# VectorE writes the inverse of the softmax totals itself, over all columns that carry it

## The chip, the cores and the metric

The kernel runs on one core of a Trainium2 chip. The metric is the device time of one execution in microseconds (us). Several executions are timed, and the median is given. One further execution is recorded by the profiler; all durations in this text come from that one.

## What is computed

The input x has 4 batches of 1024 positions with 256 values each, in fp32. Four blocks follow one another, each with a layer norm before it and a residual sum behind it: attention, a feed-forward network, a second attention, and the same feed-forward network again.

```python
x = x + _L0_attn_a_ref(_layernorm(x), kernel, WO)
x = x + _L0_ffn_ref(_layernorm(x), w1, b1, w2, b2)
x = x + _L0_attn_b_ref(_layernorm(x), w_down_q, w_down_kv, w_up_q, w_up_k, w_up_v, w_out, ln_scale, ln_bias)
x = x + _L0_ffn_ref(_layernorm(x), w1, b1, w2, b2)
```

Both attentions have 16 heads of 64 values and full rows of 1024 scores:

```python
scores = jnp.einsum('bhsd,bhtd->bhst', q, k) * scale
attn = jax.nn.softmax(scores, axis=-1)
out = jnp.einsum('bhst,bhtd->bhsd', attn, v)
```

The first makes q, k and v straight from the normed x. The second goes through two projections to 128 values, rotates q and k, and has a second norm. The softmax is what the change touches: each row of exponentials has to be divided by its total.

## The kernel before, in words

**Tiles.** Heads are worked on in pairs, and a pair of one batch takes 8 steps (`NT`), each of 128 positions as queries. With 4 batches and 8 pairs that is 256 steps for each attention layer, 512 in all. In one step there are two score tiles of 128 x 1024 (j = 0 and 1), in PSUM; the pool `ps_sc` has three such tiles. Score tile j holds the 128 queries of the pair's head j, one to a partition.

**One step, by engine.** TensorE makes the scores (`scores`, L247). VectorE takes each row's maximum, negated (`exponentials`, L258, two instructions a step). ScalarE makes the exponentials into the tile p and adds up each row's total into `total`, a tile of 128 x 2 (L260). The tile p has 17 groups (`NK`) of 128 columns: 16 carry exponentials, and the last one, p[:, NK2], carries the inverse of the totals, 64 columns for each of the two score tiles. `invert` fills that group: VectorE inverts the two totals in place (L268), and ScalarE copies each of them over its 64 columns (L269, read with a repeated element). Then VectorE transposes all 2176 columns of p in blocks of 32 x 32 into the tile T (`turn`, L280). Because the inverses are columns of p, they are transposed and moved together with the exponentials, and arrive lying along the axis along which they have to multiply.

**After the step.** Two steps (`HB`) share one T, called h. Its 16 blocks of 32 partitions are sent to their places in the tile pT by DMAs (`send`, L304): five are issued by GpSimd, the others by SyncE; SyncE has eleven per h in the first layer and ten in the second, where one block that need not change its partitions is copied by ScalarE instead (`keep`, L296). Five steps (`LAG`) later `weigh` (L313) multiplies pT by v on TensorE, `take` copies the sums to oT (ScalarE, L323) and multiplies them by the inverses that came along in pT (GpSimd, L325), and `project` (L176, L335, L337) applies the output weights and adds the result to x.

**Order.** The order on every engine is written out by hand in `steps_with`. In step s the program issues: `invert(s)`, `scores(s + 1)`, GpSimd's sends or `project` of an earlier h, the first maximum and exponentials of s + 1, other pieces of work that have a due step (projections of the next heads, norms), `weigh`, the second maximum and exponentials of s + 1, `take`, `turn(s)`, SyncE's sends. So VectorE's queue reads, step after step: inverse of s, two maxima of s + 1, transposition of s. Each engine works through its own queue in that order and waits at an instruction until what it needs is there. p, T and pT have two buffers each.

Between the two attention layers and at the end lie the feed-forward networks, which do not use `invert`.

The lines that the text names: L140 and L145 invert the spread of the norms (reciprocals of 128 x 4 to 128 x 24), L147 multiplies tiles of the same sizes by -1, L247 scores, L258 maxima, L260 exponentials, L268 and L269 the inversion, L280 the transposition, L304 the sends, L313 the weighing.

Of the kernel before, what the change touches and what calls it, by code (L numbers as in the profile page):

```python
# [48 lines left out]
def hybrid_block_kernel(  # L49
# [5 lines left out]
    nc = tc.nc  # L55
# [134 lines left out]
    def attention(prep_batch, prep_pair, wo, loader, lead, kept):  # L190
# [74 lines left out]

        def invert(s):
            t = total.pop(s)
            nc.vector.reciprocal(t, t)  # L268
            nc.scalar.copy(  # L269
                probs[s][:, NK2].rearrange("p (j c) i -> p j (c i)", j=2),  # L270
                t.unsqueeze(2).to_broadcast([P, 2, DH]),
            )
# [66 lines left out]
        def steps_with(others):  # L339
            for k, f in others:  # L340
                pieces.setdefault(k, []).append(f)
            for s in range(-1, n + LAG + 1):
                h, part = divmod(s - LAG, HB)
                ahead = 0 <= s + 1 < n
                if 0 <= s < n:
                    invert(s)
                if ahead:
                    scores(s + 1)
                if part == 1 and 0 <= s // HB - 1 < n // HB:
                    send(s // HB - 1, nc.gpsimd, sent[len(sent) - POOL_DMA :])  # L350
                if part == 1 and 0 <= h < n // HB:
                    project(h)
                if ahead:
                    exponentials(s + 1, 0)
                for f in pieces.get(s - EARLY, ()):
                    f()
                if part == 0 and 0 <= h < n // HB:
                    weigh(h)
                if ahead:
                    exponentials(s + 1, 1)  # L360
                if part == 0 and 0 <= h < n // HB:
                    take(h)
                if 0 <= s < n:
                    turn(s)
                if part == 0 and 0 <= s // HB - 1 < n // HB:
                    keep(s // HB - 1)
                    T.pop(s // HB - 1)
                if part == 0 and 0 <= s < n:
                    send(s // HB, nc.sync, sent[: len(sent) - POOL_DMA])
                for f in pieces.get(s, ()):  # L370
                    f()
# [597 lines left out]
```

## Time and profile before

| | |
|---|---|
| median of 3 runs | 3253.63 us (3250.37 to 3256.33) |
| the profiled execution | 3250.15 us, of which the span from first to last instruction is 3248.4 |
| granted TensorE clock | 0.996 of full speed |
| VectorE | 2723.5 us busy (84%), 2686 instructions |
| ScalarE | 2137.9 us busy (66%), 4400 instructions |
| TensorE | 3164.4 us busy (97%) |
| the inversion on VectorE (L268) | 512 x 130 ns = 66.7 us |
| the copy on ScalarE (L269) | 512 x 297 ns = 151.9 us |

PE is TensorE's matmul, PEld its loading of weights, DVE is VectorE, ACT ScalarE, POOL GpSimd, SP SyncE (its queue, SPq, issues DMAs). A group's row names the line, the engine, the operation, output<-inputs with shapes, and how often it occurs; then the busy time in us and the mean of one in ns; then how long the engine idled just before these instructions and what ended most of that idle time. Matmul times are modelled, so a busy TensorE is not necessarily one at its peak.

### The profile page before, as it was taken

To read this page: it belongs to the slowest core of one execution; us is meant where nothing else is said; L and a number is where in the kernel's file an instruction comes from. 1 tells how busy PE (TensorE), PEld (TensorE's weight loads), DVE (VectorE), ACT (ScalarE), POOL (GpSimd) and SP (SyncE) were. 2 spreads that over 40 slices of the span, in tenths; PEclk is the share of its full clock that TensorE was granted. 3 is DMA by queue.
4 is the path that set the end of the run, shared out by engine and by line. 5 is a ranking of instruction groups with operands and counts; after the bars stand their busy time and mean duration, and the time that the engine had idled before them with its cause. 6 is when DMAs were issued, how large, how long until landed. Compare 5 with 4: busy or idle time off the path is not lost.

```text
span 3248.4 us, 128967 instructions
## 1 busy us (share of the span) xinstructions
PE 3164.4 (97%) x53648; PEld 2092.2 (64%) x53648; DVE 2723.5 (84%) x2686; ACT 2137.9 (66%) x4400; POOL 2002.1 (62%) x2782
## 2 busy tenths in 40 slices
PE   8999999999999999999999999999999999999999
PEld 4666666666666666668866566666666666655688
DVE  7988888888888888966569989998999999999554
ACT  5666666666666666655447777777778777777542
POOL 4544545455444545442249889899899889886311
PEclk9999999999999999999999999999999999999999
DMA  8888888888888888850029889988989899988200
GB/s 228 217 224 215 224 224 228 217 219 222 221 217 225 219 231 223 221 150 1 4 74 244 225 228 243 242 237 236 246 243 243 234 240 246 238 235 221 57 20 27
DMA packets 244709, 642.29 MB, mean 198 GB/s; under 512 B 74304, under 2 KB 102976, under 8 KB 244128
## 3 DMA queue, kind: packets, MB, share of 16 engines
q1 hardware_dynamic: 161104, 397.60, 48.0%
q0 software_dynamic: 83024, 236.44, 26.0%
q8 instruction: 426, 6.98, 1.0%
q14 instruction: 155, 1.27, 0.1%
HBM read 43.39 MB, written 4.19 MB: 15 GB/s over the span
## 4 chain that ended last, share of the span: by engine, by line
PE 69%; SPq 12%; DMA 6%; DVE 5%; ACT 4%; issue 3%; POOL 1%; DVEq 0%; ACTq 0%; POOLq 0%
PE sc L247 20%; PE mm L313 19%; PE mm L176 15%; SPq L304 11%; DMA pT<-T 5%; PE pw L495 4%; PE mm L185 4%; PE mm L495 3%; PE mm L615 2%; DVE T L280 2%; DVE nmax L258 1%; ACT p L260 1%; PE ph L604 1%; ACT gT L529 1%; PE mm L162 1%
## 5 line engine op out<-in xcount | busy, mean ns | idle before, releaser
L258 DVE TENSOR_REDUCE nmax<-sc 128x1 f32<-128x1024 f32 x1024 | 1204.5, 1218 | 214.3 <-PE sc L247 211.3
L260 ACT ACTIVATE p<-sc,nmax 128x1024 f32<-128x1024 f32 x1024 | 1145.3, 1119 | 322.3 <-DVE nmax L258 322.2
L280 DVE STREAM_TRANSPOSE T<-p 128x2176 f32<-128x2176 f32 x512 | 1247.3, 2436 | 48.4 <-DMA pT<-T 18.4
L247 PE MATMUL sc<-kT,qT 64*64 64x512 f32 x8192 | 1082.5, 598 | 11.9 <-ACT p L260 10.3
L313 PEld LDWEIGHTS mm<-pT,v 64*64 64x64 f32 x32768 | 949.5, 133 | 140.7 <-issue 98.5
L313 PE MATMUL mm<-pT,v 64*64 64x128 f32 x32768 | 983.0, 269 | 9.6 <-issue 8.5
L304 POOL DMA_DIRECT2D pT<-T x1280 | 629.6, 499 | 125.5 <-PE sc L247 57.7
L325 POOL TENSOR_TENSOR oT<-oT,pT 128x256 f32<-128x256 f32 x256 | 187.0, 730 | 696.3 <-ACT oT L323 623.0
L247 PEld LDWEIGHTS sc<-kT,qT 64*64 64x64 f32 x8192 | 332.8, 133 | 401.6 <-issue 274.5
L337 POOL TENSOR_TENSOR x<-x,got 128x512 f32<-128x512 f32 x256 | 331.0, 1293 | 25.8 <-ACT got L335 22.0
L335 ACT COPY got<-mm 128x512 f32<-128x512 f32 x256 | 150.0, 586 | 281.8 <-PE mm L176 281.8
L176 PE MATMUL mm<-wo,oT 128*64 128x256 f32 x2048 | 279.9, 394 | 24.1 <-POOL oT L325 22.8
L176 PEld LDWEIGHTS mm<-wo,oT 128*64 128x64 f32 x2048 | 124.9, 136 | 273.2 <-POOL oT L325 226.5
L269 ACT COPY p<-total 128x128 f32<-128x128 f32 x512 | 151.9, 297 | 198.6 <-DVE total L268 192.4
L176 PE MATMUL mm<-hT,w 128*64 128x512 f32 x1024 | 243.4, 597 | 0.9 <-ACT hT L165 0.9
L260 ACT ACTIVATION_READ_ACCUMULATOR p<-sc,nmax 128x1 f32 x1024 | 205.2, 200 | 0.0
L185 PEld LDWEIGHTS mm<-w,hT 128*64 128x64 f32 x4096 | 140.9, 138 | 71.3 <-issue 69.4
L871 POOL TENSOR_TENSOR turned<-turned,sin_sb 128x512 f32<-128x512 f32 x128 | 163.8, 1279 | 0.0
L409 POOL TENSOR_TENSOR x<-x,b_sb 128x256 f32<-128x256 f32 x64 | 48.8, 777 | 170.6 <-ACT xn L156 170.6
L296 ACT COPY pT<-T 32x1088 f32<-32x1088 f32 x128 | 140.3, 1096 | 4.9 <-DMA pT<-T 1.1
L185 PE MATMUL mm<-w,hT 128*64 128x64 f32 x4096 | 140.9, 222 | 0.2 <-ACT kT L758 0.2
L176 PEld LDWEIGHTS mm<-hT,w 128*64 128x64 f32 x1024 | 73.3, 138 | 96.8 <-issue 75.0
(145 smaller groups left out, 2928.5 us busy)
## 6 DMA issues: line engine op xcount, KB each, us to landing
pT<-T SPq DMA_DIRECT2D x2688, 136.0 KB, 4.7
pT<-T POOLq DMA_DIRECT2D x1280, 136.0 KB, 4.7
turned<-kT POOLq DMA_DIRECT2D x128, 128.0 KB, 3.4
turned<-qT POOLq DMA_DIRECT2D x128, 128.0 KB, 3.5
w<-in_wqkv_a POOLq DMA_DIRECT2D x96, 128.0 KB, 6.0
wo<-in_wo_a POOLq DMA_DIRECT2D x32, 128.0 KB, 5.4
wo<-in_wo_a POOLq DMA_DIRECT2D x64, 64.0 KB, 5.5
wo<-in_wo_b SPq DMA_DIRECT2D x32, 128.0 KB, 4.0
```

The source lines that it names most:

```text
L176: nc.tensor.matmul(out[ts(j, DH)], lhsT[:, ts(j, DH)], rhs[j], start=(first and i == 0), stop=(last and i == len(parts) - 1),)
L185: nc.tensor.matmul(out[ts(j, DH)], lhsT, rhs[:, ts(j, DH)], start=(i == 0), stop=(i == len(parts) - 1),)
L247: nc.tensor.matmul(sc[s, j][ts(half, DH), ts(m, 512)], qT()[rows, ts(2 * qs + half, DH)], kT()[rows, ts(m, 512)], start=True, stop=True,)
L258: nc.vector.tensor_reduce(nmax, sc[s, j], AX.X, ALU.max, negate=True)
L260: nc.scalar.activation(probs[s][:, :NK2, ts(j, 2), :], sc.pop((s, j)).rearrange("p (k c i) -> p k c i", c=2, i=SQ), AF.Exp, bias=nmax, acc ...
L280: nc.vector.transpose(T[h][:, :, q, :, :].rearrange("p c k i -> p k c i"), probs.pop(s))
L304: engine.dma_start(pT[h][ts(c, SQ), a], T[h][ts(a, SQ), c])
L313: nc.tensor.matmul(av[h][q][ts(j ^ q, DH)], v[ts(j, DH), k, :], pT[h][ts(j, DH), :, q, k, :], start=(k == 0), stop=(k == NK2 - 1),)
L325: nc.gpsimd.tensor_mul(parts, parts, pT.pop(h)[:, :, :, NK2, :])
L337: nc.gpsimd.tensor_add(xd, xd, got)
L495: nc.tensor.matmul(bank[:, t, : right(k).shape[-1]], left(t, k), right(k), start=(first and t == 0 and k == 0), stop=(k == n_k - 1), skip_ ...
L871: nc.gpsimd.tensor_mul(other, other, sin_sb[:, ts(qb, QB)])
```

## The change

The reciprocal no longer overwrites the 128 x 2 tile of totals. It reads that tile with each element repeated 64 times and writes its results straight into the 128 columns of p. ScalarE's copy is gone.

```diff
         def invert(s):
             t = total.pop(s)
-            nc.vector.reciprocal(t, t)
-            nc.scalar.copy(
+            nc.vector.reciprocal(
                 probs[s][:, NK2].rearrange("p (j c) i -> p j (c i)", j=2),
                 t.unsqueeze(2).to_broadcast([P, 2, DH]),
             )
```

The place of the reciprocal in VectorE's queue is the same. Lines behind the change have numbers that are smaller by one.

## The prediction

> **What bounds the kernel now.** I read the page's busy table and chain first, then VectorE's groups by shape, then the two attention stages cut out as windows, and last VectorE's order of time inside them.
>
> ```profile
> span 3248.4 us, 128967 instructions
> PE 3164.4 (97%) x53648; PEld 2092.2 (64%) x53648; DVE 2723.5 (84%) x2686; ACT 2137.9 (66%) x4400; POOL 2002.1 (62%) x2782
> PE 69%; SPq 12%; DMA 6%; DVE 5%; ACT 4%; issue 3%; POOL 1%; DVEq 0%; ACTq 0%; POOLq 0%
> L269 ACT COPY p<-total 128x128 f32<-128x128 f32 x512 | 151.9, 297 | 198.6 <-DVE total L268 192.4
> ```
>
> TensorE leads, but VectorE has 84% over the whole span and ScalarE only 66%. The change takes work from the engine with room and may give some to the one with little. The chain gives VectorE 5% now; that tells what a small saving there is worth, not what more work there costs.
>
> The windows run from the first to the last inversion of each attention layer (columns: stretch, its length, then busy time and instructions of PE, PEld, DVE, ACT and POOL, then clock and DMA):
>
> ```profile
> 28.20:1419.16 1390.96, 1382.19 (x26335) 869.87 (x26328) 1230.69 (x1091) 898.58 (x1944) 682.20 (x1068) 1.00 0.86 220
> 1668.40:3009.40 1341.00, 1304.49 (x23968) 823.29 (x23960) 1224.86 (x1064) 1020.78 (x2039) 1174.18 (x1529) 0.99 0.88 235
> ```
>
> VectorE is 1230.69/1390.96 = 88% busy in the first layer, 91% in the second. It has 160.3 and 116.1 us of idle time left, over 256 steps each: 0.63 and 0.45 us a step. The granted clock is 1.00 and 0.99, so no stall hides in it.
>
> The order of time shows where the idle time lies (start, length, what; in brackets the idle time before). First two steps of the first layer, then two of the second:
>
> ```profile
> 1002.70 0.12 DVE L268 RECIPROCAL total<-total 128x2 f32<-128x2 f32 x1
> 1003.28 2.35 DVE L258 TENSOR_REDUCE nmax<-sc 128x1 f32<-128x1024 f32 x2 [0.46 <-PE sc L247]
> 1005.55 2.43 DVE L280 STREAM_TRANSPOSE T<-p 128x2176 f32<-128x2176 f32 x1
> 1007.91 0.12 DVE L268 RECIPROCAL total<-total 128x2 f32<-128x2 f32 x1
> 1009.40 2.35 DVE L258 TENSOR_REDUCE nmax<-sc 128x1 f32<-128x1024 f32 x2 [1.37 <-PE sc L247]
> 1011.67 2.43 DVE L280 STREAM_TRANSPOSE T<-p 128x2176 f32<-128x2176 f32 x1
> ```
>
> ```profile
> 2406.62 0.12 DVE L268 RECIPROCAL total<-total 128x2 f32<-128x2 f32 x1
> 2407.20 2.36 DVE L258 TENSOR_REDUCE nmax<-sc 128x1 f32<-128x1024 f32 x2 [0.46 <-PE sc L247]
> 2410.12 2.45 DVE L280 STREAM_TRANSPOSE T<-p 128x2176 f32<-128x2176 f32 x1 [0.57 <-DMA w<-in_wuq]
> 2412.49 0.12 DVE L268 RECIPROCAL total<-total 128x2 f32<-128x2 f32 x1
> 2412.54 2.33 DVE L258 TENSOR_REDUCE nmax<-sc 128x1 f32<-128x1024 f32 x2
> 2414.79 2.43 DVE L280 STREAM_TRANSPOSE T<-p 128x2176 f32<-128x2176 f32 x1
> ```
>
> A step is one reciprocal, two maxima and one transposition, about 4.8 us of VectorE. The idle time sits just behind the reciprocal, where the maxima wait for TensorE's scores: a longer reciprocal first eats that wait. In the first layer nearly every step has one. In the second, every other step has none: the step from 2412.49 goes straight through, and 114 of its 255 steps idle under 0.1 us.
>
> **The change part by part.**
>
> *Removed: ScalarE's copy (L269).* 512 x 0.297 = 151.9 us of ScalarE and its 192.4 us of waiting for the inverse. That ScalarE was late is rare: the maxima's results are what its exponentials wait for (322.2 us, 259 times), and the transposition waited for this copy 4.5 us in all, 2 times. I count the removal at 0; its cover is the 2.36 us of maxima between inverse and transposition. Bounds: 0 and 4.5 us of gain.
>
> *Changed: the reciprocal now writes 128 columns instead of 2.* No row has a reciprocal of 128 columns, nor one that reads a repeated operand. The nearest are those of the same operation, type and memory:
>
> ```profile
> L140 DVE RECIPROCAL a_rstd<-a_rstd 128x4 f32<-128x4 f32 x2 | 0.4, 178 | 0.7 <-ACT a_rstd L139 0.7
> L140 DVE RECIPROCAL f_rstd<-f_rstd 128x8 f32<-128x8 f32 x2 | 0.4, 202 | 1.6 <-ACT f_rstd L139 1.6
> L140 DVE RECIPROCAL f_rstd<-f_rstd 128x16 f32<-128x16 f32 x1 | 0.3, 253 | 14.3 <-ACT f_rstd L139 14.3
> L140 DVE RECIPROCAL a_rstd<-a_rstd 128x24 f32<-128x24 f32 x1 | 0.3, 303 | 1.6 <-ACT a_rstd L139 1.6
> L147 DVE TENSOR_SCALAR a_shift<-a_shift 128x24 f32<-128x24 f32 x1 | 0.2, 178 | 0.0
> ```
>
> From 4 to 24 columns the time grows by 125 ns: 6.25 ns a column. The straight line 153 + 6.25 n meets all four rows within 1 ns. The multiplication of the same 24 columns took 178, and the one of 8 took 171, so it is the reciprocal itself that is slow per element. At 128 columns the line gives 303 + 104 x 6.25 = 953 ns for one that starts after a wait. The 2-column one took 167 at most after a wait and 124 in the median, directly behind another instruction; so 908 is an estimate for the back-to-back form. Added per step: 126 x 6.25 = 0.79 us. Bounds: 0.78 (908 less the mean of 130) and 0.83 (953 less 120) if the line holds. The lower end if it does not is a rate like the multiplication's, 0.45 ns a column: 0.06 us. I take 0.79, since the rows of the same operation are nearest.
>
> A rule of the Trainium skill makes this dearer still. The page "VectorE: DVE Perf Modes", section "Walkthrough: the 8-slice pipeline in each mode", says that the reciprocal is an iterative divide with a repeat count of 8. Read as 8 cycles a column at its 0.96 GHz, that would be 8.33 ns and 1.05 us more per step, where the rows show 6.25 ns; by it the sum below would be about 270 us. I go by the rows.
>
> *Moved or queued behind it.* The order on VectorE stays: inverse, two maxima, transposition. Behind the longer inverse stand the maxima, behind them ScalarE's exponentials, and then TensorE, which may not write new scores before the exponentials have freed a score tile (three tiles). No DMA is added or moved on a queue; SyncE's and GpSimd's transfers of T start later by as much as the transposition ends later. The transposition no longer waits for ScalarE.
>
> *The sum.* All 512 cost 512 x 0.79 = 403 us of VectorE; the question is how much falls into its idle time.
> - Floor: VectorE never idles again. First layer 1230.69 + 256 x 0.7875 = 1432.3, 41.3 over its length; second 1224.86 + 201.6 = 1426.5, 85.5 over. Together 127 us.
> - Ceiling: each step has only its own idle time. I take each stretch from one L268 to the next and subtract VectorE's rows in it, overlap once; what idle time falls short of 0.7875 is added. That gives 59 and 117: 176 us.
> - Taken: TensorE can work ahead by about one step (with three score tiles it may write the next scores as soon as the first exponential of the current step is done), so a step with much TensorE work can borrow from the light one before it, but no further. The same sum over pairs of steps (1.575 us against the idle time of both) gives 51 and 97: 148 us.
>
> The sum goes on the profiled execution: 3250.15 + 148 = 3398. The median of three was 3253.63, 3.5 above that execution, within the runs' own spread (3250.37 to 3256.33); I say 3400.
>
> **Rivals.**
> 1. *TensorE can't work ahead.* Then each step pays alone: +176 us, with 0.83 us per step +193: 3426 to 3444. For it: in the first layer TensorE is busy 99%, so both engines are near their limit and any jitter of one stalls the other. Against it: the three score tiles.
> 2. *The repeated read, or the other tile as output, slows each column.* Such a thing is in the trace: VectorE's subtractions of 128x1024 at L422 take 1434 ns and the additions of that shape at L420 1219, 18% more for other operands. 18% on 6.25 ns is 7.4 ns, 0.93 us a step: by pairs 83 + 130 = 213, so 3463. Against it: the reciprocal's rate is already far below the one at which VectorE reads or writes here.
> 3. *Not slower: the repeated operand goes through at nearly the rate of a copy.* Place: L268's slope. From the pair sums, an addition of 0.20 us a step costs 5 us, so below about 0.2 us (1.6 ns a column) the waits for scores swallow it; at 0.06 us nothing is left of it, and the 4.5 us that the transposition waited for ScalarE are won: 3246 to 3250. For it: no row shows a repeated operand. Against it: the slope of the multiplication is 0.45 ns, that of every reciprocal 6.25.
> 4. *The freed ScalarE pays for it.* It can't: the floor is made of VectorE's own busy time, and no wait on ScalarE can be shorter than none.
>
> **How the numbers follow.** Forecast 0.70, rival 1 0.18, rival 2 0.06, rival 3 0.04; 0.02 is for a slope in between. The low end is the floor at 0.78 us (512 x 0.78 less 276 of idle time, 123 us, 3373) less the 4.5 us of ScalarE and the spread of runs: 3362. The high end is rival 1 at 0.83 us, 3444, plus the upper half of that spread and a few us for the ramps: 3455. That leaves out rivals 2 and 3 and parts of 1. A measurement of this kernel tells about 0.2% (6.5 us) from no change. Slower: 0.95; within 0.2%: 0.03 (most of rival 3); faster: 0.02.
>
> **What would show it right or wrong.** In the profile after: L268 as a 128x128 group of about 0.91 us and 466 us busy; no copy of total on ScalarE; VectorE near 97% busy in both attention stages, and 5.6 us between inversions in both; the maxima's 211 us of waiting for scores mostly gone; TensorE's share lower, with waits for exponentials or maxima instead; SyncE's transfers out of the chain of the second layer. If L268 lasts 0.9 us but VectorE still idles over 0.25 us a step, rival 1 is right. If L268 is about 0.2 us, the whole forecast falls; if it is over 1.1, it is too low.

## The result and the profile after

The changed kernel takes 3345.96 us (median of 4 runs, 3343.72 to 3347.45), the kernel before in the same comparison 3254.98. The ratio is 1.0281, with a 95% interval of 1.0268 to 1.0294: slower, by 91 us. The forecast was slower by 146 us, with 3362 as its low end; the measured time lies 16 us below that.

First the row of the maxima in the kernel before, then lines of the changed kernel's page: its span, the engines' busy time, the chain, and the groups of the maxima and of the inversion. Line numbers behind the change are smaller by one.

```profile
L258 DVE TENSOR_REDUCE nmax<-sc 128x1 f32<-128x1024 f32 x1024 | 1204.5, 1218 | 214.3 <-PE sc L247 211.3
```

```profile
span 3343.2 us, 128081 instructions
PE 3220.1 (96%) x53648; PEld 2118.6 (63%) x53648; DVE 3061.3 (92%) x2686; ACT 1986.5 (59%) x3888; POOL 2001.1 (60%) x2782
PE 42%; DVE 26%; SPq 14%; DMA 10%; ACT 4%; issue 3%; POOL 1%; DVEq 0%; ACTq 0%; POOLq 0%
L258 DVE TENSOR_REDUCE nmax<-sc 128x1 f32<-128x1024 f32 x1024 | 1174.1, 1188 | 23.8 <-PE sc L247 23.2
L268 DVE RECIPROCAL p<-total 128x128 f32<-128x128 f32 x512 | 469.9, 918 | 12.5 <-ACT p L260 10.8
```

The reciprocal of 128 columns takes 918 ns in the mean. The maxima waited 211 us for TensorE's scores before and wait 23 us now. VectorE's share of the chain rises from 5% to 26%. One figure does not fit a sum in which every other instruction keeps its cost: the 1024 maxima cost 1204.5 us before and 1174.1 now, though nothing about them was changed.

The two attention stages as windows, each again from the first inversion to the last (columns: stretch, length, then busy time and instructions of PE, PEld, DVE, ACT, POOL, then clock and DMA):

```profile
27.32:1445.10 1417.78, 1397.58 (x26334) 877.36 (x26328) 1399.05 (x1091) 816.74 (x1689) 681.24 (x1068) 1.00 0.84 216
1693.24:3103.05 1409.81, 1345.26 (x23968) 844.31 (x23960) 1392.63 (x1064) 951.84 (x1784) 1174.15 (x1528) 1.00 0.85 223
```

VectorE is busy for 1399.05 of 1417.78 us and for 1392.63 of 1409.81: 99% in both layers. The first layer grew by 26.8 us and the second by 68.8, together 95.6, and the whole span by 94.8, so the rest of it adds nothing. The granted clock is 1.00 in both layers, against 1.00 and 0.99 before.

VectorE's order of time in the second layer:

```profile
2405.76 2.43 DVE L279 STREAM_TRANSPOSE T<-p 128x2176 f32<-128x2176 f32 x1
2408.12 0.91 DVE L268 RECIPROCAL p<-total 128x128 f32<-128x128 f32 x1
2408.95 2.29 DVE L258 TENSOR_REDUCE nmax<-sc 128x1 f32<-128x1024 f32 x2
2411.16 2.43 DVE L279 STREAM_TRANSPOSE T<-p 128x2176 f32<-128x2176 f32 x1
2413.51 0.91 DVE L268 RECIPROCAL p<-total 128x128 f32<-128x128 f32 x1
```

From one reciprocal to the next there are 5.39 us and no gap. Such a step without a wait I call a clean step below. The shortest of before took 4.65 us (90 of the second layer's 255 steps take under 4.72). Each row starts some 0.08 us before the record of the row ahead of it ends: instructions that follow one another directly overlap.

### The profile page after: what moved, and what is told of

The parts are those of the page before. It is cut to its first block, busy times and chain, and to the rows that moved or that the text cites. A ratio compares the mean times of both kernels' runs of the same rounds, so it can differ in the third digit from the quotient of the medians.

```text
span 3343.2 us, 128081 instructions
## 1 busy us (share of the span) xinstructions
PE 3220.1 (96%) x53648; PEld 2118.6 (63%) x53648; DVE 3061.3 (92%) x2686; ACT 1986.5 (59%) x3888; POOL 2001.1 (60%) x2782
## 4 chain that ended last, share of the span: by engine, by line
PE 42%; DVE 26%; SPq 14%; DMA 10%; ACT 4%; issue 3%; POOL 1%; DVEq 0%; ACTq 0%; POOLq 0%
SPq L303 13%; DVE T L279 12%; PE sc L247 11%; PE mm L312 10%; DVE nmax L258 9%; DMA pT<-T 8%; PE mm L176 8%; PE pw L494 4%; PE mm L494 3%; DVE p L268 3%; PE mm L185 3%; PE mm L614 2%; ACT p L260 1%; PE ph L603 1%; ACT gT L528 1%
## 5 line engine op out<-in xcount | busy, mean ns | idle before, releaser
L258 DVE TENSOR_REDUCE nmax<-sc 128x1 f32<-128x1024 f32 x1024 | 1174.1, 1188 | 23.8 <-PE sc L247 23.2
L247 PE MATMUL sc<-kT,qT 64*64 64x512 f32 x8192 | 1144.7, 601 | 28.1 <-ACT p L260 26.0
L312 PEld LDWEIGHTS mm<-pT,v 64*64 64x64 f32 x32768 | 967.7, 133 | 128.3 <-issue 87.2
L312 PE MATMUL mm<-pT,v 64*64 64x128 f32 x32768 | 999.5, 269 | 13.3 <-issue 12.3
L247 PEld LDWEIGHTS sc<-kT,qT 64*64 64x64 f32 x8192 | 350.8, 132 | 456.1 <-issue 275.5
L268 DVE RECIPROCAL p<-total 128x128 f32<-128x128 f32 x512 | 469.9, 918 | 12.5 <-ACT p L260 10.8
```

The costliest lines, as they stand in the source:

```text
L247: nc.tensor.matmul(sc[s, j][ts(half, DH), ts(m, 512)], qT()[rows, ts(2 * qs + half, DH)], kT()[rows, ts(m, 512)], start=True, stop=True,)
L258: nc.vector.tensor_reduce(nmax, sc[s, j], AX.X, ALU.max, negate=True)
L268: nc.vector.reciprocal(probs[s][:, NK2].rearrange("p (j c) i -> p j (c i)", j=2), t.unsqueeze(2).to_broadcast([P, 2, DH]),)
L312: nc.tensor.matmul(av[h][q][ts(j ^ q, DH)], v[ts(j, DH), k, :], pT[h][ts(j, DH), :, q, k, :], start=(k == 0), stop=(k == NK2 - 1),)
```

## The experiments

Each diff is against the kernel before, except where the text names another; lines that only make a spare tile are left out of the diffs.

Theory after the result: VectorE's time is the bound, and the kernel's time follows VectorE's clean step, whatever that step contains. The loss was smaller than forecast because VectorE's other instructions take less time once nothing makes them wait. Main rival: the work taken off ScalarE did win something back.

### The same VectorE work, with ScalarE's copy put back

```diff
-            nc.vector.reciprocal(t, t)
+            wide = wides[s % 2]
+            nc.vector.reciprocal(wide, t.unsqueeze(2).to_broadcast([P, 2, DH]))
             nc.scalar.copy(
-                probs[s][:, NK2].rearrange("p (j c) i -> p j (c i)", j=2),
-                t.unsqueeze(2).to_broadcast([P, 2, DH]),
+                probs[s][:, NK2].rearrange("p (j c) i -> p j (c i)", j=2), wide
             )
```

> VectorE makes the same 128-column reciprocal as in the changed kernel, but into a spare tile, and ScalarE copies it into p as it did before. So VectorE's work is that of the changed kernel and ScalarE's that of the old one. Theory (VectorE's time is the bound; what made the loss smaller than forecast is that VectorE's other instructions get shorter when nothing waits): 3346 us within 10, ratio to before 1.025 to 1.032, idle time of VectorE about 0.07 us a step. Rival (the freed ScalarE won back the missing 55 us): 3390 to 3405, and VectorE idle for 0.15 us a step or more.

Measured: 3349.65 us, ratio 1.0297 [1.0280, 1.0314]; the interval overlaps that of the changed kernel. The engines' busy time:

```profile
PE 3223.2 (96%) x53648; PEld 2120.6 (63%) x53648; DVE 3063.4 (91%) x2686; ACT 2135.7 (64%) x4400; POOL 2001.1 (60%) x2782
```

ScalarE is busy for 2135.7 us, about as before, 149 us more than in the changed kernel, and VectorE idles for 0.08 us a step. ScalarE's relief is worth at most a few us. The rival falls.

### Other VectorE work of the same length

```diff
             nc.vector.reciprocal(t, t)
+            nc.vector.tensor_reduce(
+                spare[:, s % 2], ident[:, :116].unsqueeze(1).to_broadcast([P, 6, 116]), AX.XY, ALU.max
+            )
             nc.scalar.copy(
```

> The kernel before, with its 2-column reciprocal and its copy on ScalarE, and behind each reciprocal one more VectorE instruction that nobody needs: a maximum over 696 columns of a constant tile, about 0.79 us when it follows directly. Theory (only the added VectorE time matters, whatever it is spent on): 3346 us within 12, clean steps of 5.39 us. Rival (the loss comes from the reciprocal itself: its place before the write of p, the transposition that must wait for it): less than half of the loss, under 3300.

Measured: 3366.88 us, ratio 1.0355 [1.0340, 1.0371], 21 us more than the changed kernel and outside what I expected. Its clean step is 5.43 us instead of 5.39, and 512 x 0.04 = 20 us. The row of the step's own maxima in this run:

```profile
L259 DVE TENSOR_REDUCE nmax<-sc 128x1 f32<-128x1024 f32 x1024 | 1200.4, 1213 | 20.7 <-PE sc L248 20.1
```

They cost 1200.4 us here and 1174.1 in the changed kernel, and that is where the 0.04 us lie; the added instruction is not too long. If only the time is counted that is not overlapped by the instruction ahead, reciprocal and added maximum come to 421.5 us over 510 steps, 0.83 us a step, and the changed kernel's reciprocal to 431.2, 0.85 a step. But a first maximum directly behind the added one adds 1.13 us to the step, and one directly behind the wide reciprocal 1.08. So VectorE work that has nothing to do with p costs at least as much, and the reciprocal's output or the wait for it are not needed to explain the loss. That the loss was not larger still has in part to do with what stands ahead of the maximum.

### Half of the columns

```diff
-            nc.vector.reciprocal(t, t)
-            nc.scalar.copy(
-                probs[s][:, NK2].rearrange("p (j c) i -> p j (c i)", j=2),
-                t.unsqueeze(2).to_broadcast([P, 2, DH]),
-            )
+            to = probs[s][:, NK2].rearrange("p (j c) i -> p j c i", j=2)
+            nc.vector.reciprocal(to[:, :, 0], t.unsqueeze(2).to_broadcast([P, 2, SQ]))
+            nc.scalar.copy(to[:, :, 1], to[:, :, 0])
```

> The reciprocal writes 64 of the 128 columns of p, and ScalarE copies them to the other 64. By 6.25 ns a column it lasts about 0.51 us directly behind another instruction, 0.39 more than before. Theory (idle time is used up first, and freely across steps): no idle time is exhausted in the first layer, the second nearly: 3250 to 3265, ratio 1.000 to 1.005. Rival (each step pays alone): 12 and 46 us from the per-step sums of the trace before: about 3310.

Measured: 3272.28 us, ratio 1.0066 [1.0051, 1.0081]. The group's row of this run:

```profile
L269 DVE RECIPROCAL p<-total 128x64 f32<-128x64 f32 x512 | 264.5, 517 | 25.5 <-ACT p L260 22.9
```

64 columns take 517 ns and 128 take 918: 401 ns for 64 columns, 6.27 ns each. The time lies between the two theories: 20 us lost, where free sharing of idle time gave at most 0.5% (16 us) and steps that pay alone 58. The profiled execution is the slowest of the four (3279.38 us) and 29 us above the profiled one of before; the pair sum that the prediction used gives 30 for this addition. VectorE still idles 0.31 and 0.23 us a step in the two layers, so it is not the only limit here; half of the added time cost between a fifth and a third of the loss.

### VectorE does the copy as well

```diff
             nc.vector.reciprocal(t, t)
-            nc.scalar.copy(
+            nc.vector.tensor_copy(
```

> VectorE makes the 2-column reciprocal and then copies it over the 128 columns of p itself; ScalarE's copy is gone as in the changed kernel. The copy is estimated at 0.14 to 0.22 us from the 24-column multiplication (178 ns, 0.45 ns a column). Theory (ScalarE's relief is worth nothing, the small addition falls into idle time): 3250 to 3270, same as before within 0.5%. Rival (ScalarE's relief is worth some 55 us): 3195 to 3230, faster than before.

Measured: 3412.31 us, ratio 1.0490 [1.0474, 1.0506], slower than the changed kernel, whose reciprocal takes four times as long as a short one of these copies. Both theories fell here. The group of the copies, and VectorE's order of time in the second layer:

```profile
L269 DVE COPY p<-total 128x128 f32<-128x128 f32 x512 | 300.1, 586 | 17.5
```

```profile
2403.02 0.23 DVE L269 COPY p<-total 128x128 f32<-128x128 f32 x1
2403.16 2.35 DVE L258 TENSOR_REDUCE nmax<-sc 128x1 f32<-128x1024 f32 x2
2405.43 2.43 DVE L280 STREAM_TRANSPOSE T<-p 128x2176 f32<-128x2176 f32 x1
2407.79 0.12 DVE L268 RECIPROCAL total<-total 128x2 f32<-128x2 f32 x1
2407.94 2.39 DVE L269 COPY p<-total 128x128 f32<-128x128 f32 x1
```

The same copy takes 0.23 us in one step and 2.39 in the next. GpSimd's order of time at that place:

```profile
2407.75 1.27 POOL L870 TENSOR_TENSOR kT<-kT,cos_sb 128x512 f32<-128x512 f32 x1
2408.97 1.26 POOL L871 TENSOR_TENSOR turned<-turned,sin_sb 128x512 f32<-128x512 f32 x1
2410.32 1.27 POOL L872 TENSOR_TENSOR kT<-kT,turned 128x512 f32<-128x512 f32 x1
```

The long copy ends at 2410.33, and GpSimd's second multiplication at 2410.23. It is so each time: of the 512 copies 109 take over 0.4 us, 106 of them in the second layer, where GpSimd rotates q and k, and every one of the 109 ends 0.08 to 0.10 us behind the end of a GpSimd tensor instruction. The excess of all copies over 0.227 us adds up to 184 us; the run is 160 us slower than the kernel before. By these times the copy waits for GpSimd; the next run tests it.

### The same spreading by a maximum over one element

```diff
             nc.vector.reciprocal(t, t)
-            nc.scalar.copy(
+            nc.vector.tensor_reduce(
                 probs[s][:, NK2].rearrange("p (j c) i -> p j (c i)", j=2),
-                t.unsqueeze(2).to_broadcast([P, 2, DH]),
+                t.unsqueeze(2).unsqueeze(3).to_broadcast([P, 2, DH, 1]), AX.X, ALU.max,
             )
```

> As the run in which VectorE makes the 2-column reciprocal and spreads it itself, but the spreading is a maximum over one element each (128 outputs) instead of a copy. In that run the copies took 0.23 us except for 109 that took up to 4.2 us and ended 0.08 to 0.10 us after a GpSimd tensor instruction. Theory (the copy alone has to wait for GpSimd's access to SBUF, a maximum does not; VectorE's added time is then about 0.2 us and falls into idle time): no spreading instruction over 0.4 us, 3248 to 3270. Rival (any VectorE instruction at that place waits for GpSimd): over 3350.

Measured: 3278.41 us, ratio 1.0065 [1.0049, 1.0081]. The group:

```profile
L269 DVE TENSOR_REDUCE p<-total 128x128 f32<-128x128 f32 x512 | 146.4, 286 | 17.5
```

All 512 take 285 to 289 ns, against 226 to 4198 for the copy at the same place with the same operands, though 98 of them lie wholly within a GpSimd multiplication or addition. So here the copy waits for GpSimd and the maximum does not. The time is 8 us above what I expected: the clean step is 4.98 us, 0.33 more than before. That is more than the 0.29 of the instruction, since it starts 0.03 us after the reciprocal ends and does not overlap it. That clean step is the one of the half-width run (4.99 us), and so is the ratio: 1.0065 and 1.0066.

### The wide reciprocal twice

This diff is against the changed kernel.

```diff
             nc.vector.reciprocal(
                 probs[s][:, NK2].rearrange("p (j c) i -> p j (c i)", j=2),
                 t.unsqueeze(2).to_broadcast([P, 2, DH]),
             )
+            nc.vector.reciprocal(wides[s % 2], t.unsqueeze(2).to_broadcast([P, 2, DH]))
```

> The changed kernel, and in every step the 128-column reciprocal a second time, into a spare tile. VectorE is already saturated there (clean steps of 5.39 us, idle 0.07 us a step). Theory (once nothing waits, VectorE's instructions can't get shorter any more, so more work is paid in full): 0.834 us a step, clean steps of 6.22 us, 512 x 0.834 = 427 us less at most the 36 us of idle time that is left: 3737 to 3780. Rival (instructions go on getting shorter, or other slack is found, as with the first reciprocal, where only 92 of 403 us were paid): under 3650.

Measured: 3723.41 us, ratio 1.1432 [1.1415, 1.1450]: 377 us more than the changed kernel. The order of time in the first layer:

```profile
1004.98 0.91 DVE L269 RECIPROCAL p<-total 128x128 f32<-128x128 f32 x1
1005.81 0.90 DVE L273 RECIPROCAL wide<-total 128x128 f32<-128x128 f32 x1
1006.62 2.29 DVE L259 TENSOR_REDUCE nmax<-sc 128x1 f32<-128x1024 f32 x2
1008.82 2.44 DVE L281 STREAM_TRANSPOSE T<-p 128x2176 f32<-128x2176 f32 x1
```

The clean step is 6.20 us: the second reciprocal adds 0.81, not 0.834, because it overlaps the first. The first 0.79 us per step cost 91 us; the next 0.81 cost 377. 512 x 0.81 = 415, of which 25 us went into idle time that was left (36 us in the changed kernel, 11 now). Of the other 13 us, 8 are the step's maxima, which took that much less once more (counted without overlap), and 2 the transpositions. The 14 us below my lower bound are mostly this overlap.

### The wide reciprocal between the two maxima

This diff, too, is against the changed kernel.

```diff
-                if 0 <= s < n:
-                    invert(s)
                 if ahead:
                     scores(s + 1)
...
                 if ahead:
                     exponentials(s + 1, 0)
+                if 0 <= s < n:
+                    invert(s)
```

> The changed kernel with its 128-column reciprocal issued between the two maxima of the next step. VectorE's work is the same, but the first maximum, and so ScalarE and TensorE, get going 0.83 us earlier in each step. Theory (VectorE's own time is the bound): at most the remaining 36 us of idle time can be won, 3315 to 3350. Rival (what counts is the delay of the first maximum and of the scores behind it): most of the loss goes, under 3300.

Measured: 3393.04 us, ratio 1.0414 [1.0394, 1.0433], 47 us slower than the changed kernel. Neither theory allowed for a loss of this size. The order of time in the first layer, where 38 of the 47 us lie, with only the rows of the chain that the text follows:

```profile
1001.84 1.11 ACT L260 ACTIVATE p<-sc,nmax 128x1024 f32<-128x1024 f32 x1 [0.67 <-DVE nmax L258]
1002.95 0.42 ACT L322 COPY oT<-mm 128x128 f32<-128x128 f32 x2
1003.45 0.72 POOL L324 TENSOR_TENSOR oT<-oT,pT 128x256 f32<-128x256 f32 x1 [7.53 <-ACT oT L322]
1004.23 1.08 PE L176 MATMUL mm<-wo,oT 128*64 128x256 f32 x8 [0.42 <-POOL oT L324]
1006.86 1.10 PE L185 MATMUL mm<-w,hT 128*64 128x64 f32 x32
1007.89 1.95 PE L247 MATMUL sc<-kT,qT 64*64 64x512 f32 x16
1009.89 1.23 DVE L258 TENSOR_REDUCE nmax<-sc 128x1 f32<-128x1024 f32 x1 [0.34 <-PE sc L247]
```

The clean step is still 5.39 us, but every other step of the first layer takes 5.84 in the median: the first maximum waits for scores again (85 us in all instead of 23). TensorE reaches these scores only behind the projection, which waits for GpSimd's product, which waits for ScalarE's copy of oT, which stands behind the second exponential of the step. With the reciprocal ahead of both maxima, its 0.83 us lie between the transposition and the moment at which scores are needed; between the maxima they do not. That it is this chain I read from the rows; no run removed it.

### The cheap spreading between the two maxima

```diff
-                if 0 <= s < n:
-                    invert(s)
                 if ahead:
                     scores(s + 1)
...
                 if ahead:
                     exponentials(s + 1, 0)
+                if 0 <= s < n:
+                    invert(s)
```

This diff is against the run that spreads by a maximum.

> The same, with the inversion issued between the two maxima of the next step instead of ahead of both. In the kernel before, the 2-column reciprocal waited for ScalarE's exponentials in 57 of the second layer's steps (0.24 us each); behind the first maximum it should not wait, and the maximum gets its result out earlier. Theory: 5 to 20 us faster than with the inversion ahead, 3235 to 3260; it is the candidate to beat the kernel before. Rival (TensorE and the transfers bound these steps anyway): no difference from the inversion ahead of both, within 0.2%.

Measured: 3289.11 us, ratio 1.0100 [1.0085, 1.0115], 11 us slower than with the inversion ahead. The reciprocal no longer waits for ScalarE (25.0 us of idle time before it, now 0.0), but the maxima wait for scores for 130 us instead of 98.5. So the gain that I expected did not come. Whether it is the chain of the run above is not shown: VectorE's idle time in the two layers is nearly the same in both orders (177.2 us ahead, 172.9 between), and the profiled executions are only 5.5 us apart. No run beat the kernel before.

## Why the prediction was wrong

**What held.**
- *The price of the reciprocal.* The line 153 + 6.25 n, from rows of 4 to 24 columns, gave 953 ns after a wait and 908 directly behind another instruction. Measured: 955 at most and 911 in the median. The reciprocals grew by 399.5 us over 510 steps, against 402 expected. The difference of the two medians, 911 - 124 over 126 columns, is 6.25 ns a column. The prediction's estimate from the Trainium skill's page "VectorE: DVE Perf Modes", section "Walkthrough: the 8-slice pipeline in each mode", whose repeat count of 8 it read as 8 cycles a column, was 8.33 ns; the trace does not bear that reading out.
- *ScalarE's removal at 0.* The run with the copy put back agrees within 4 us.
- *VectorE as the new bound,* 99% busy, steps of 5.56 and 5.53 us (5.6 was forecast), the maxima's wait for scores mostly gone (23 of 211 us are left).
- Rivals 1, 2 and 3 did not come.

One of the signs did not come either: SyncE's transfers were to leave the chain of the second layer, but SPq has 14% of the whole chain now, against 12.

**What failed: the floor in the sum, by its premise that VectorE's other instructions keep their time.** It took VectorE's busy time of before, 1230.69 and 1224.86 us, as work that stays, and added 201.6 to each. The pair sum, which gave the forecast, and the ceiling rest on the same premise, since they set the addition against idle time alone. The measured loss, 95 us between the profiled executions, is below even the floor's 127. Rival 4 was dismissed with this floor; ScalarE's relief was indeed worth next to nothing, but that is shown by the run with the copy put back and not by the floor. The busy time of the other instructions was not fixed: the windows of after show 1399.05 and 1392.63, 67 us less than the floor's 1432.3 and 1426.5. Adding up, for each VectorE instruction between the first and the last inversion of each layer, only the time that is not overlapped by the one ahead of it:

| instructions | before, us | after, us | change |
|---|---|---|---|
| reciprocals of the totals | 31.7 | 431.2 | +399.5 |
| first maxima | 612.3 | 557.7 | -54.6 |
| second maxima | 577.0 | 574.0 | -3.0 |
| transpositions | 1206.6 | 1201.0 | -5.6 |
| idle time | 276.4 | 35.9 | -240.5 |
| sum of these | | | +95.8 |

The maxima and transpositions took 63 us less, 55 of them at the first maxima. A first maximum that started behind a wait added 1.225 us; one directly behind the 2-column reciprocal 1.12 in the median (1.134 in the mean); one directly behind the 128-column reciprocal 1.08. Before, 373 of 510 stood behind a wait, after 34. So two things share the 55 us. Some 31 us are the waits that went: 339 times the 0.09 us by which a maximum behind a wait exceeded one directly behind the short reciprocal. The other 24 us are 0.05 us for each of the 476 that now stand directly behind a wide reciprocal. Its length is not the reason: behind the half-width run's reciprocal of 64 columns it is 1.08 as well, and 1.13 behind a maximum, be it the 0.29 us one that spreads or the 0.85 us one of the run with other work. Why it depends on the kind of instruction ahead stays open.

**A smaller error the other way.** The pair sum left 21 us of idle time (148 less 127); 36 remained. So the forecast's 148 us less 63, less 3.5 for reciprocals that cost 399.5 instead of 403, plus these 15, comes to about 96, where the layers grew by 95.6. The half-width run shows both errors at work: for its 0.39 us a step the pair sum leaves 107 us of idle time and 136 remained, while the maxima took 27 us less than before. There the two nearly cancel, and that the pair sum's 30 us agree with the profiled execution's 29 is luck.

**How it could have been read.** The clean steps of before stood in the trace. 4.65 + 0.79 is 5.44 for a saturated step; times 510, plus 28 us of other VectorE work in the two layers, is 2802, which is 70 over the two layers' 2732. With the 21 us of idle time that the pair sum left this gives +91, and with the 36 that were found afterwards +106: 3341 to 3356 on the profiled execution, which took 3344.98. It would have been close partly by luck: the clean step came out at 5.39 and not 5.44, 25 us less, and the steps that were not clean cost 14 us more besides their idle time.

## What to carry to other kernels

Ask what an engine's step costs when nothing waits, and read it from steps that have no wait, not from the mean busy time: here a first maximum added 1.225 us behind a wait and 1.08 to 1.13 directly behind another instruction. An instruction moved to the engine that is nearly full is first paid from its idle time and then in full: here the first 0.79 us per step cost 91 us and the next 0.81 cost 377. Repeating a value before a slow operation, instead of after it, multiplies the slow operation: the reciprocal has 6.25 ns a column, where a maximum's spreading of all 128 takes 0.29 us.

## What the runs showed of the hardware that was not expected

- A VectorE copy between tiles in SBUF can wait for GpSimd: 226 ns alone, up to 4198 when GpSimd has tensor instructions running, each of the 109 long ones ending 0.08 to 0.10 us behind one of them. A maximum and a reciprocal with the same operands are not held (285 to 289 ns and 904 to 955). The Trainium skill has this in "GPSIMD Engine Reference", section "Specifications": its access to SBUF is shared with VectorE, with contention for VectorE instructions in a two-port mode. The trace agrees in that the copy was held and the maximum was not; the time of the held copies adds up to 184 us. That the copy ran in such a mode no run shows directly.
- The Trainium skill's page "VectorE: DVE Perf Modes", in its section on the perf-mode tier table, gives such a copy a double rate that a reduction does not have. The rows agree in sense (226 against 286 ns), but in this kernel the faster form was by far the dearer one, 3412.31 us against 3278.41.
- A maximum over 1024 columns adds 1.225 us to its step behind a wait, 1.13 directly behind another maximum (of 0.29 or 0.85 us), 1.12 behind a 2-column reciprocal, and 1.08 behind a reciprocal of 64 or 128 columns. It goes by the kind of the instruction ahead and not by its length; why is open.
